# Other PSUM banks for the early softmax scores, and two softmax items a step at the end, in a fused attention, retention and feed-forward kernel

## The chip, the cores and the metric

The kernel runs on one core of a Trainium2 chip, in float32 throughout. The metric is the time on the device for one call, in microseconds (us); lower is better.

## The reference

The input is `x` with 8 sequences of 512 tokens and 256 features. Four blocks follow each other, each of them `x = x + block(layernorm(x))`: an attention with 16 heads of 16 features, a feed-forward layer (256 to 1024, relu, back to 256), a retention (scores times a decay mask, no softmax), and the same feed-forward layer again. The attention is the part that the change touches:

```python
att = jnp.einsum('bhqd,bhkd->bhqk', q, k) / jnp.sqrt(jnp.float32(HEAD_DIM))
...
att = att + (log_sparse + jnp.log(decay + 1e-09))[None, None]
att = jax.nn.softmax(att, axis=-1)
out = jnp.einsum('bhqk,bhkd->bhqd', att, v)
...
out = out + 0.2 * infini_out
```

`log_sparse` and `decay` depend on the distance of query and key alone. `q` and `k` are rotated (rope), and `k` and `v` come through a latent of 64 features.

## The kernel before, in words

The attention of one sequence is cut into four groups of four heads, so there are 32 groups. Each group is cut into 8 items: an item is 128 rows of a pair of heads against all 512 columns. That makes 256 items, and each is computed twice.

- The score item `s` has queries in rows. Two matmuls (`score_item`, L449) fill one tile of two PSUM banks, and VectorE takes the maximum of each row from it (`reduce_item`, L462, output `mr`). When a group's 8 items are through, `shift` (L470) turns the maxima with a TensorE transpose (`mx`), ScalarE negates them (`neg`), and a DMA from ScalarE's queue writes them into a spare row of `qT`.
- The softmax item `t` has keys in rows. Two matmuls (`prob_item`, L480) compute the same scores with the maximum already subtracted. ScalarE takes the exponential into a tile `p` in SBUF (`soft_item`, L493), and the tile is multiplied there with the table `dec_a` of the distance terms, half by half: on GpSimd for every third item, else on VectorE. Four such `p` tiles exist.
- `pv_item` (L504) multiplies the two items of one row block (both pairs of heads) with the values. The values carry a column of ones, so that the sum of the softmax comes out with it.

PSUM has eight banks: two score tiles `sc` of two banks each, which `s` and `t` share, one bank for `pv`, and three general banks (`misc`, L203) for everything else: layernorm transposes, latent, rope inputs, transposes of the maxima (`mx`) and of the attention's output (`num`, `aT`), output projection `wo`, feed-forward `hx` and `x`, retention `b`, `bv`, `bs`, `bo`.

One step of the main loop runs score item `t` and softmax item `t - LAG` (LAG is 10) in one burst of four matmuls, which lie on four different groups of 32 rows of TensorE. Ahead of the burst of every odd step from 13 on stands the `pv` of the two items that came last but one and last but two. The heads of an odd item are the first of that `pv`. After step 255 ten steps remain that have a softmax item alone.

All other matmul work is cut into units (class `Unit`, L280), each with a price for TensorE (`pe`) and for the engines behind it (`then`). They form chains: the front half of each sequence (layernorm, latent, k, q, rope, gates, values) and the rest of it (output projection, feed-forward, retention, feed-forward). A planner at the end of the kernel goes through the steps and decides, with clocks of its own for each engine, what stands between two steps: a unit is issued ahead of a step if it can start by the time the step can, and if a credit, which spreads the remaining work over the remaining steps, isn't used up. Its clocks only set the order. TensorE executes strictly in the order that the planner writes, as do the DMAs of the queue SP; the other engines' order within their queues is set by a scheduler from the same program. Engines wait for each other through semaphores.

The planner's own bookkeeping of the score tiles is `behind`: a step waits in the plan for the last maximum and the last exponential. The `pv` of a step is counted when the step is issued, not when it is asked when the step can start.

The early steps have little other work: the output projection of the first sequence can only start when its four groups are through, at about step 44.

## Time and profile before

| | |
|---|---|
| median of 3 runs | 1386.85 us (1384.02 to 1388.44) |
| the profiled execution | 1393.77 us |
| its span, first to last instruction | 1391.9 us |
| granted TensorE clock, mean | 0.96 |
| TensorE matmuls busy | 1286.9 us (92%) |
| VectorE busy | 805.7 us (58%) |
| ScalarE busy | 452.6 us (33%) |
| GpSimd busy | 390.5 us (28%) |

The page names instructions by what they write and read: `mr<-s` is the maximum of a score tile, `p<-t` the exponential, `p<-p,dec_a` the product with the distance table, `pv<-p,va` the product with the values. All instructions of VectorE, ScalarE and GpSimd carry line L69 and all matmuls L198 or, for transposes, L201, because small helpers issue them; so groups are told apart by tile names. `PE` is TensorE, `PEld` its weight loads, `DVE` VectorE, `ACT` ScalarE, `POOL` GpSimd, `SP` the engine that issues most DMAs. The granted clock is the share of full speed that TensorE was given.

From the page's groups of instructions, with the number of instructions, busy time and mean length of one:

| group | count | busy us | mean ns |
|---|---|---|---|
| VectorE maximum, 128x1024 | 256 | 312.7 | 1221 |
| ScalarE exponential, 128x1024 | 256 | 261.9 | 1023 |
| VectorE product with `dec_a`, 128x512 | 342 | 228.6 | 709 |
| GpSimd product with `dec_a`, 128x512 | 170 | 213.4 | 1277 |
| matmuls of `s` | 1024 | 305.6 | 680 |
| matmuls of `t` | 1024 | 301.8 | 666 |
| matmuls of `pv` | 1024 | 148.8 | 627 |

Matmul records overlap where they run on different row groups, and each float32 matmul has two records.

### The profile page before, as it was taken

To read this page: it belongs to the slowest core of one execution; us is meant where nothing else is said; L and a number is where in the kernel's file an instruction comes from. 1 tells how busy PE (TensorE), PEld (TensorE's weight loads), DVE (VectorE), ACT (ScalarE), POOL (GpSimd) and SP (SyncE) were. 2 spreads that over 40 slices of the span, in tenths; PEclk is the share of its full clock that TensorE was granted. 3 is DMA by queue.
4 is the path that set the end of the run, shared out by engine and by line. 5 is a ranking of instruction groups with operands and counts; after the bars stand their busy time and mean duration, and the time that the engine had idled before them with its cause. 6 is when DMAs were issued, how large, how long until landed. Compare 5 with 4: busy or idle time off the path is not lost.

```text
span 1391.9 us, 15456 instructions
## 1 busy us (share of the span) xinstructions
PE 1286.9 (92%) x6116; PEld 629.3 (45%) x6116; DVE 805.7 (58%) x1335; ACT 452.6 (33%) x612; POOL 390.5 (28%) x449
## 2 busy tenths in 40 slices
PE   6887799888989899898999999999999999999998
PEld 3221234343534353444535445445445454556675
DVE  4578665674584585545866667555766466524130
ACT  2133424324233324343242432433333333332211
POOL 5133341331231252213333234222432133122010
PEclk9699979998989999999999999999999999999999
DMA  5430120001200011001200030001200000000000
GB/s 130 134 62 1 27 51 1 1 1 31 47 16 1 20 36 24 16 1 31 47 1 1 5 73 16 1 0 34 44 1 1 8 8 1 1 12 4 0 16 16
DMA packets 22158, 32.08 MB, mean 23 GB/s; under 512 B 2987, under 2 KB 12652, under 8 KB 21806
## 3 DMA queue, kind: packets, MB, share of 16 engines
q1 hardware_dynamic: 21446, 30.83, 9.5%
q8 instruction: 48, 0.79, 0.2%
q10 hardware_dynamic: 640, 0.26, 0.1%
q14 instruction: 24, 0.20, 0.0%
HBM read 18.24 MB, written 12.58 MB: 22 GB/s over the span
## 4 chain that ended last, share of the span: by engine, by line
PE 66%; DVE 11%; POOL 4%; issue 3%; ACT 1%; DMA 0%; POOLq 0%; DVEq 0%; ACTq 0%
PE hx L198 15%; PE x L198 15%; PE s L198 13%; PE pv L198 6%; DVE mr L69 4%; PE wo L198 2%; PE b L198 2%; PE bs L198 2%; PE bv L198 2%; PE t L198 1%; DVE x L69 1%; PE q L198 1%; DVE p L69 1%; PE bo L198 1%; POOL p L69 1%
## 5 line engine op out<-in xcount | busy, mean ns | idle before, releaser
L69 DVE TENSOR_REDUCE mr<-s 128x2 f32<-128x1024 f32 x256 | 312.7, 1221 | 257.9 <-PE t L198 242.0
L69 ACT ACTIVATE p<-t 128x1024 f32<-128x1024 f32 x256 | 261.9, 1023 | 501.5 <-PE t L198 451.2
L69 POOL TENSOR_TENSOR p<-p,dec_a 128x512 f32<-128x512 f32 x170 | 213.4, 1277 | 545.6 <-ACT p L69 471.0
L198 PE MATMUL s<-kT,qT 32*128 32x512 f32 x1024 | 305.6, 680 | 53.2 <-DVE mr L69 48.7
L198 PE MATMUL t<-qT,kT 32*128 32x512 f32 x1024 | 301.8, 666 | 5.1 <-ACT p L69 3.8
L69 DVE TENSOR_TENSOR p<-p,dec_a 128x512 f32<-128x512 f32 x342 | 228.6, 709 | 42.6 <-ACT p L69 42.5
L198 PE MATMUL x<-w_sb,h_x 128*128 128x256 f32 x1024 | 237.2, 387 | 0.0
L198 PEld LDWEIGHTS x<-w_sb,h_x 128*128 128x128 f32 x1024 | 191.9, 191 | 61.0 <-issue 33.6
L198 PEld LDWEIGHTS s<-kT,qT 32*128 32x128 f32 x1024 | 81.7, 193 | 231.5 <-DVE mr L69 113.6
L198 PE MATMUL pv<-p,va 128*32 128x512 f32 x1024 | 148.8, 627 | 1.3 <-POOL p L69 1.1
L69 ACT ACTIVATE h_x<-hx,vec 128x512 f32<-128x512 f32 x128 | 87.8, 687 | 147.6 <-PE hx L198 146.8
L198 PE MATMUL hx<-xT_g,w_sb 128*128 128x512 f32 x256 | 122.4, 620 | 1.7 <-ACT xT_g L69 1.7
L198 PE MATMUL hx<-xT_f,w_sb 128*128 128x512 f32 x256 | 118.7, 601 | 1.2 <-ACT xT_f L69 1.1
L69 DVE TENSOR_TENSOR x<-x,x 128x256 f32<-128x256 f32 x64 | 27.1, 424 | 148.7 <-PE x L198 148.7
L198 PEld LDWEIGHTS t<-qT,kT 32*128 32x128 f32 x1024 | 79.8, 189 | 17.6 <-ACT p L69 9.2
L198 PEld LDWEIGHTS hx<-xT_g,w_sb 128*128 128x128 f32 x256 | 47.3, 195 | 68.1 <-issue 57.5
L198 PEld LDWEIGHTS hx<-xT_f,w_sb 128*128 128x128 f32 x256 | 45.5, 190 | 59.0 <-issue 52.3
L69 POOL TENSOR_TENSOR x<-x,row 128x256 f32<-128x256 f32 x64 | 54.1, 864 | 17.9 <-DVE xn_f L69 9.5
L69 POOL TENSOR_TENSOR rc<-rc,rs 128x512 f32<-128x512 f32 x32 | 39.9, 1268 | 65.0 <-DVE rc L69 48.4
L198 PEld LDWEIGHTS pv<-p,va 128*32 128x32 f32 x1024 | 22.0, 109 | 76.6 <-issue 41.8
L69 POOL TENSOR_SCALAR ve_r<-mv_r 128x2 f32<-128x2 f32 x16 | 3.6, 223 | 137.8 <-DVE mv_r L69 137.8
L198 PE MATMUL b<-xT_r,ct 128*128 128x512 f32 x64 | 32.5, 642 | 6.4 <-ACT xT_r L69 6.4
(130 smaller groups left out, 1071.6 us busy)
## 6 DMA issues: line engine op xcount, KB each, us to landing
dk<-rc SPq DMA_DIRECT2D x16, 256.0 KB
kT<-dk SPq DMA_DIRECT2D x32, 128.0 KB
dq<-rc SPq DMA_DIRECT2D x16, 256.0 KB
qT<-dq SPq DMA_DIRECT2D x32, 128.0 KB
out_dram<-x SPq DMA_DIRECT2D x32, 128.0 KB
x<-in_x_dram SPq DMA_DIRECT2D x7, 512.0 KB
w_sb<-in_w_dram SPq DMA_DIRECT2D x2, 1024.0 KB
x<-in_x_dram SPq DMA_DIRECT2D x2, 256.0 KB
```

Source lines behind the costliest of these rows:

```text
L69: ins = f(*a, **k)
L198: tc.keep_in_program_order(nc.tensor.matmul(o, lhsT=l, rhs=r, start=start, stop=stop))
```

## The change

The first 34 softmax items (`EARLY`) no longer use the score tiles. Their two matmuls write two general banks (`misc`), and ScalarE takes the exponential of each half by itself. In these steps both score tiles are free for the row maxima. Of these 34 items every even one is multiplied on GpSimd, and the odd ones on VectorE; later items are divided as before.

The ten softmax items that follow the last score item are issued two to a step, so five steps of four matmuls take the place of ten with two.

The planner's bookkeeping follows: a queue `sc` of two times stands for the two score tiles, a list `steps` gives for each step its score item, its softmax items and the item whose `pv` it carries, `step_start` now counts the wait of a `pv`, and the price of a VectorE product goes from 1680 to 1500. The order of everything that follows is planned anew with these clocks.

```diff
+    EARLY = PER + 2
...
+    def on_pool(n):
+        return n % 2 == 0 if n < EARLY else n % 3 == 2
...
-        ps = ps_sc.tile([P, 2, T], F32, tag="sc", name=f"t_{n}")
+        if n < EARLY:
+
+            ps = [misc(f"t{e}_{n}") for e in range(2)]
+        else:
+            both = ps_sc.tile([P, 2, T], F32, tag="sc", name=f"t_{n}")
+            ps = [both[:, e, :] for e in range(2)]
+            ps.append(both)
...
-        act.activation(p, ps, AF.Exp, scale=0.25)
+        if n < EARLY:
+            for e in range(2):
+                act.activation(p[:, e, :], ps[e], AF.Exp, scale=0.25)
+        else:
+            act.activation(p, ps[2], AF.Exp, scale=0.25)
...
-        eng = gps if n % 3 == 2 else dve
+        eng = gps if on_pool(n) else dve
...
+    sc = deque([0, 0])
+    steps = [(t, [t - LAG] if t >= LAG else [], t - LAG - PVLAG) for t in range(NS)]
+    steps += [(None, [n, n + 1], n - 1) for n in range(NS - LAG, NS, 2)] + [(None, [], NS - 1)]
...
     def step_start(t):
-        s = clock["PE"]
-        if t < NS:
-            s = max(s, behind["s"])
-        n = t - LAG
-        if 0 <= n < NS:
-            s = max(s, behind["t"])
-            if shifted[n // 8].done is None:
+
+        s, ts, _ = steps[t]
+        n = values_of(t)
+        at_ = clock["PE"]
+        if n is not None:
+            at_ = max(at_, prob_at[n] - 100, prob_at[n - 1] - 100)
+        own = 0
+        need = (s is not None) + sum(i >= EARLY for i in ts)
+        if need:
+            own = sc[need - 1]
+        for i in ts:
+            if i < EARLY:
+                own = max(own, banks[1])
+            if shifted[i // 8].done is None:
                 return None
-            s = max(s, shifted[n // 8].done + 2300)
-        return s
+            own = max(own, shifted[i // 8].done + 2300)
+        return max(at_, own - (1000 if n is not None else 0))
...
+            prob_at[i] = clock[e] = max(clock[e], clock["ACT"] + 60) + (2700 if on_pool(i) else 1500)
...
-    LAST = NS + LAG + PVLAG
+    LAST = len(steps)
```

More of the change, by code (lines that the diff above doesn't have):

```diff
@@ L483, in prob_item @@
         b, g = divmod(i, NG)
-        ps = ps_sc.tile([P, 2, T], F32, tag="sc", name=f"t_{n}")
+        if n < EARLY:
[4 more added lines that the diff above has]
+            ps.append(both)
         return ps, [
             (
-                ps[:, e, :], kT[b % 2][h * 32 : h * 32 + 32, g, t * P : (t + 1) * P],
+                ps[e], kT[b % 2][h * 32 : h * 32 + 32, g, t * P : (t + 1) * P],
                 qT[b % 2][h * 32 : h * 32 + 32, g, :],
@@ L724, in tile_kernel @@
     held = []
-    behind = {"s": 0, "t": 0}
-    maxed, shifted, prob_at, out_at = {}, {}, {}, {}
+    sc = deque([0, 0])
+    maxed, shifted, prob_at = {}, {}, {}
+    steps = [(t, [t - LAG] if t >= LAG else [], t - LAG - PVLAG) for t in range(NS)]
+    steps += [(None, [n, n + 1], n - 1) for n in range(NS - LAG, NS, 2)] + [(None, [], NS - 1)]
     def start_of(u):
@@ L770, in shift_unit, with values_of @@
         return u
+    def values_of(t):
+        n = steps[t][2]
+        return n if n > 0 and n % 2 == 1 else None
     def step_start(t):
-        s = clock["PE"]
-        if t < NS:
-            s = max(s, behind["s"])
-        n = t - LAG
-        if 0 <= n < NS:
-            s = max(s, behind["t"])
-            if shifted[n // 8].done is None:
-                return None
-            s = max(s, shifted[n // 8].done + 2300)
-        return s
+        s, ts, _ = steps[t]
[11 more added lines that the diff above has]
+            if shifted[i // 8].done is None:
+                return None
+            own = max(own, shifted[i // 8].done + 2300)
+        return max(at_, own - (1000 if n is not None else 0))
     def step(t):
-        n = t - LAG - PVLAG
-        if 0 <= n < NS and n % 2 == 1:
+        s, ts, _ = steps[t]
+        at_ = step_start(t)
+        n = values_of(t)
+        if n is not None:
             pv_item(n)
-            clock["PE"] = max(clock["PE"], prob_at[n], prob_at[n - 1], out_at.get(n // 8 - 1, 0)) + 1000
+            at_ += 1000
             if n % 8 == 7:
@@ L791, in step @@
                 made = Unit(None)
-                made.done = clock["PE"] + 100
+                made.done = at_ + 100
                 us[0].after.append(made)
                 posts.extend(us)
-        at_ = step_start(t)
         mms, after = [], []
-        if t < NS:
-            ps, m = score_item(t)
+        if s is not None:
+            ps, m = score_item(s)
             mms += m
-            after.append((reduce_item, t, ps))
-        n = t - LAG
-        if 0 <= n < NS:
-            ps, m = prob_item(n)
+            after.append((reduce_item, s, ps))
+        for i in ts:
+            ps, m = prob_item(i)
             mms += m
-            after.append((soft_item, n, ps))
+            after.append((soft_item, i, ps))
         for o, l, r in mms:
@@ L808, in step @@
         if mms:
-            clock["PE"] = at_ + 1080
+            at_ += 1080
+        clock["PE"] = at_
         for f, k, ps in after:
             f(k, ps)
-        if t < NS:
-            behind["s"] = maxed[t] = clock["DVE"] = max(clock["DVE"], clock["PE"] + 100) + 1280
-            if t % 8 == 7:
-                posts.append(shift_unit(t // 8))
-        if 0 <= n < NS:
-            behind["t"] = clock["ACT"] = max(clock["ACT"], clock["PE"] + 100) + 1090
-            e = "POOL" if n % 3 == 2 else "DVE"
-            prob_at[n] = clock[e] = max(clock[e], behind["t"] + 60) + (2700 if n % 3 == 2 else 1680)
+        if s is not None:
+            maxed[s] = clock["DVE"] = max(clock["DVE"], at_ + 100) + 1280
+            sc.popleft()
+            sc.append(maxed[s])
+            if s % 8 == 7:
+                posts.append(shift_unit(s // 8))
+        for i in ts:
+            if i < EARLY:
+                for e in range(2):
+                    clock["ACT"] = max(clock["ACT"], at_ + 100) + 650
+                    banks.popleft()
+                    banks.append(clock["ACT"])
+            else:
+                clock["ACT"] = max(clock["ACT"], at_ + 100) + 1090
+                sc.popleft()
+                sc.append(clock["ACT"])
+            e = "POOL" if on_pool(i) else "DVE"
+            prob_at[i] = clock[e] = max(clock[e], clock["ACT"] + 60) + (2700 if on_pool(i) else 1500)
     posts = []
```

## The prediction

> **What bounds the kernel now.** I read first the windows view, with the span cut at six points: the first score, steps 10, 44 and 50 (one maximum on VectorE is one step; I counted them along the timeline, and the cut is where the step's matmuls start), the end of the scores and the last softmax item. Columns: window, its length, busy time of PE, weight loads, VectorE, ScalarE and GpSimd, granted clock, DMA share, GB/s.

> ```profile
> 37.50:64.30 26.80, 23.65 (x60) 8.00 (x57) 16.48 (x26) 2.21 (x5) 2.42 (x5) 0.59 0.43 142
> 64.30:176.70 112.40, 85.85 (x469) 25.61 (x472) 84.82 (x115) 43.53 (x56) 38.82 (x38) 0.92 0.17 34
> 176.70:210.20 33.50, 31.85 (x141) 14.32 (x133) 21.25 (x39) 8.11 (x11) 13.98 (x16) 0.82 0.22 49
> 210.20:1203.00 992.80, 939.91 (x4654) 454.60 (x4653) 619.09 (x1012) 347.55 (x459) 290.24 (x318) 0.98 0.07 16
> 1203.00:1252.00 49.00, 47.68 (x197) 23.24 (x198) 13.22 (x25) 17.71 (x22) 10.90 (x10) 1.00 0.03 9
> 1252.00:1391.90 139.90, 132.44 (x498) 89.27 (x496) 33.69 (x89) 25.50 (x40) 16.44 (x28) 0.98 0.03 9
> ```

> From 176.7 us on TensorE is 95% busy or more. The exception is the second row, steps 10 to 43: 112.4 us for 34 steps, PE 85.9, VectorE nearly as busy. What ends PE's waits there says the waits view of that window, and how a step runs says its timeline (start, length, then the instruction, and in brackets the idle time and what ended it):

> ```profile
> PE s L198 <- DVE mr L69: 20.5, 21, 3.9
> ```

> ```profile
> 119.43 0.70 PE L198 MATMUL s<-kT,qT 32*128 32x512 f32 x2 [1.31 <-DVE mr L69]
> ...
> 120.60 1.09 PE L198 MATMUL pv<-p,va 128*32 128x512 f32 x8
> 120.61 1.23 DVE L69 TENSOR_REDUCE mr<-s 128x2 f32<-128x1024 f32 x1
> 120.71 1.02 ACT L69 ACTIVATE p<-t 128x1024 f32<-128x1024 f32 x1 [1.47 <-PE t L198]
> 121.77 1.29 DVE L69 TENSOR_TENSOR p<-p,dec_a 128x512 f32<-128x512 f32 x2
> ...
> 121.89 0.70 PE L198 MATMUL s<-kT,qT 32*128 32x512 f32 x2 [0.20 <-DVE mr L69]
> ...
> 124.34 0.70 PE L198 MATMUL s<-kT,qT 32*128 32x512 f32 x2 [0.73 <-DVE mr L69]
> ```

> Bursts of s and t start 2.46 us apart. That is 1.18 to the maximum, 1.23 for it, 0.05 back: the one score tile must be read before the next burst. The burst takes PE 1.07 (121.89 to 122.96, where the next work starts), a pv 1.0. So a step without other work leaves PE idle 1.39 when no pv lies in it (odd steps) and 0.39 when one does (even): 4.92 us a pair.

> [...] two decay products take 1.29 alone, 2.03 at 87.94 us under GpSimd's rope addition. [...]

> **The change, part by part.**

> *Scores of early softmax in other banks.* Items 0 to 33 (steps 10 to 43) take two of the three general banks, and the scores for the maxima have both score tiles. The wait of s on the last maximum goes. Next in line is pv: in the order of the built program it still stands ahead of every odd burst, and it reads the product of the odd item, which is VectorE's, made behind that step's maximum. From the rows above: burst to maximum 1.18, maximum to product 1.16 (121.77 − 120.61), product 1.29, then about 1.05 until the next burst: 4.68 a pair, against 4.92. So 17 pairs × 0.24 = 4 us. Both ends: if product and GpSimd collide (+0.74, as at 87.94) the pair is 5.4, a loss of 8 us; if ScalarE and VectorE were to flow freely, PE's 3.14 a pair plus one bank wait of 0.8 would give 3.94, a gain of 17. I take 4.68, because at that time the even item's exponential is not finished yet and GpSimd still waits for it.

> *Other PE work in these steps* (k, q, v, gates, transposes, from the built orders): 16.7 us before, 18.6 after, since k of the second batch (1.98 us) moves from step 8 to 10. The gaps of 1.39 and 0.39 hide 8.1 of it now; after the change the gap ahead of pv (4.68 − 3.14, so 1.5 a pair) hides 10.7. Left open: 8.6 and 7.9. The stage of the kernel before is then 17 × 4.92 + 8.6 = 92.2, which is 20.2 short of the 112.4 measured: the low clock, statistics and rope on VectorE ahead of a maximum (steps 20 and 21 take 5.0 each), exponentials behind the key sum. These all stay, ahead of a product instead of a maximum; but the even items no longer stand behind them. I leave 14 of the 20. After: 17 × 4.68 + 7.9 + 14 = 101.5. Gain 11, and 2 more from k leaving step 8. As a check by VectorE: six items leave it, 12 × 0.707 = 8.5, the k rope comes in, 4 × 0.74 = 3.0, so 84.8 becomes 79.3; at the same 75% busy that is 105, a gain of 7. I take **10**, ends 0 and 20.

> *Exponentials in halves.* No 128x512 exponential from PSUM is in this trace. Nearest rows: the copy of num, 0.59, relu with a bias pointer, 0.69. [...] ScalarE is busy 43.5 of 112.4, the cover: zero. Bounds: [...] 0.4 us earlier first halves on GpSimd are no gain while VectorE's product ends last. The fourth matmul of a burst waits for the exponential before it (three banks, two an item), 0.8; behind it queue pv and all PE work. It lies inside the gap of 1.5: zero; 12 us if that gap were gone.

> *Decay to GpSimd.* 17 items instead of 11: 6 × 2 × 1.27 = 15 us on an engine 38.8 busy of 112.4; behind it wait rope additions and 1/std, so k and the transposes. Zero, up to 4 lost. No DMA is added; on SP the load of batch 3 moves behind q of batch 2 and some stores behind k. DMA share 0.17 and less: zero. ScalarE's own DMA of the maxima now stands behind two halves: zero, since the planner still leaves two steps.

> *After step 44.* From here each item is again in a score tile, and 2.46 is again the floor of an empty step. But the planner has the first feed-forward at step 59 instead of 50: nine more steps lie before the large matmuls and find nothing to fill them (9.3 us of other PE work in steps 44 to 49, against 16.4). Over steps 44 to 254 I set each step's other work against its gap (1.39 odd, 0.39 even): 21.4 us uncovered before, 30.8 after, of it 0.4 and 6.3 in steps 44 to 58. In before's timeline steps without other work do show medians of 1.40 and 0.39, so the price holds. **Loss 9.4**, ends 3 and 20 (odd steps with only a maxima transpose idled 1.9).

> *Last ten items, two a burst.* Four row groups instead of two in one burst: five bursts × 1.06 = 5.3 saved, and the 1.32 ahead of the burst at 1205.38 is covered. New: pv now follows one unit after its pair. Two exponentials 2.1, then VectorE's product of the second, ready at 3.7, or GpSimd's at 4.6; the units there are 2.3 (hx and a transpose), 4.0, 3.5, 3.5, 4.0. Waits 1.4, 0, 1.1, 0.5, 0: 3.0. **Net gain 3.6**, ends 1 and 6. The 140 us behind it keep their order and their work.

> **Sum.** Against the profiled execution's span: 1391.9 − 10 − 2 + 9.4 − 3.6 = 1385.7, with the 1.9 around it 1387.6. That execution, 1393.77, is 6.9 above the median of the runs, so 1380.7: **1381**, −0.4%. About 0.3%, 4 us, is what a measurement of this kernel tells from no change.

> **Rivals.**
> - *The early gain is given back (slower).* Mechanism: after step 44 PE has no large matmuls ready for nine steps more, its clock falls there as in 168 to 206 us before, and empty steps cost up to 1.9 instead of 1.39. For it: other work thins out in the built order: 48 steps from 44 on carry less than 0.9 us of it, against 26. Against: from 410 us before idled only 33 us in 800. Price: early gain 5, loss 20, last gain 2.5 and the 2 of k: +10, so **1397**. It decides from the point where the loss exceeds 16.
> - *The wait only changes its name.* The chain through pv is 4.9 or more, because product and GpSimd collide (+0.3 suffices), and early steps give nothing but the 6 us from VectorE; loss 9.4, last 3.6: **1387**. The collision at 87.94 speaks for it, the late even exponential against.
> - *The clock stays up.* 18.5 us of steps 10 to 43 ran at half clock in the kernel before; if the denser early steps hold it and stalls fall to 6 of the 20, the gain is 18 to 20, loss 5, last 4, k 2: **1366**. Against: the statistics and rope stalls keep their place.

> **Chances.** Forecast 0.45 (own range 1375 to 1387), given back 0.27, renamed 0.13, clock 0.15. Range: 1366 to 1398; it leaves out the upper part of the second and the lower of the last. Faster: 0.36 of the forecast and nearly all of the last, 0.50; same: the renamed and 0.09 of the forecast, 0.22; slower 0.28.

> **What would show it.** In steps 10 to 43: bursts in pairs of 4.7 us, the wait of s on mr gone and one of pv on p in its place, stage near 102 us; VectorE near 79 busy. Steps 44 to 58 near 50 us with the s-on-mr wait back; from the last score (1202.93) to the end of the last pv (1256.25) it is 53.3 now; 12.6 of other work leaves this stretch for earlier steps, so about 37. I am wrong if the early stage stays above 108, if 44 to 254 lose over 15, or if that stretch idles no more than before.

## The result and the profile after

The changed kernel takes 1373.0 us (median of 4 runs, 1371.7 to 1373.4) against 1385.4 for the kernel before (4 runs, one more than shown above): ratio 0.9907, 95% interval 0.9885 to 0.993. A second set of runs of the same program, told of below, gave 1373.3 and 0.9906 [0.9888, 0.9924]. That is 12 us, 0.9%, where the prediction had 0.4%. The profiled execution took 1373.4, its span is 1371.5 and its clock 0.971. The profiled execution of the kernel before had a clock of 0.960, its other runs a median of 0.968; so 1391.9 − 1371.5 = 20.4 overstates the difference of the medians by 8.

The windows view of the kernel after, from step 10 on, with the columns of the prediction. It is cut at steps 10, 44, 59 and 76, at the last score and at the end of the last `pv`; each cut at a step lies 1.18 us ahead of that step's maximum. (TensorE itself can be up to two us ahead of such a cut.)

```profile
65.40:169.80 104.40, 94.71 (x484) 31.86 (x480) 79.51 (x103) 44.45 (x88) 55.51 (x46) 0.95 0.12 26
169.80:229.80 60.00, 48.70 (x246) 18.74 (x238) 44.87 (x77) 19.72 (x26) 26.92 (x30) 0.89 0.21 45
229.80:304.50 74.70, 70.30 (x354) 31.45 (x351) 43.88 (x65) 29.90 (x43) 17.24 (x18) 1.00 0.01 3
304.50:1197.50 893.00, 850.19 (x4219) 422.05 (x4218) 548.00 (x916) 309.95 (x410) 260.77 (x293) 0.99 0.08 18
1197.50:1235.80 38.30, 37.43 (x190) 19.02 (x186) 14.87 (x21) 14.57 (x18) 11.08 (x8) 1.00 0.03 11
```

Cut in the same places, the kernel before has:

```profile
64.60:176.90 112.30, 85.75 (x468) 25.42 (x470) 84.72 (x114) 43.53 (x56) 38.52 (x38) 0.92 0.17 34
176.90:252.40 75.50, 72.82 (x338) 33.07 (x330) 47.38 (x86) 24.11 (x31) 24.21 (x28) 0.92 0.10 22
252.40:338.10 85.70, 73.26 (x350) 31.18 (x350) 49.27 (x77) 29.58 (x42) 25.12 (x26) 0.90 0.06 13
338.10:1202.90 864.80, 825.38 (x4107) 404.60 (x4106) 543.43 (x887) 301.96 (x398) 254.89 (x280) 0.98 0.08 18
1202.90:1256.30 53.40, 52.08 (x226) 26.22 (x223) 15.01 (x29) 18.54 (x23) 10.90 (x10) 1.00 0.03 9
```

Length minus PE's busy time is idle time. The early stage (first row) falls from 112.3 to 104.4 us and its idle time from 26.6 to 9.7. (Busy includes waits inside a group of matmuls: the `pv` below is shown with 1.66 us, where one that waits for nothing takes 1.06. So not all of the idle time that went became work.) Steps 44 to 58 (second row) go from 2.7 idle to 11.3: the predicted loss. Steps 59 to 75 (third row), with nearly the same number of matmuls, go from 12.4 idle to 4.4 and from a clock of 0.90 to 1.00: this was not predicted. The last row lost 15 us, most of it because 36 matmul records of other work moved ahead of it.

The waits view of the early stage of the kernel after (engine, what it waited for: us in total, times, longest):

```profile
PE pv L198 <- DVE p L69: 8.2, 3, 6.2
PE t L198 <- DVE va L69: 1.4, 1, 1.4
```

The wait of `s` on `mr`, 20.5 us before, is gone. A `pv` that waits for VectorE's product has taken its place in the list. The timeline shows it in a step without other work:

```profile
121.32 0.70 PE L198 MATMUL s<-kT,qT 32*128 32x512 f32 x2
...
122.50 1.23 DVE L69 TENSOR_REDUCE mr<-s 128x2 f32<-128x1024 f32 x1 [1.08 <-PE t L198]
...
123.25 0.29 PEld L198 LDWEIGHTS t<-qT,kT 32*128 32x128 f32 x2 [0.60 <-ACT p L69]
123.64 1.28 DVE L69 TENSOR_TENSOR p<-p,dec_a 128x512 f32<-128x512 f32 x2
124.25 3.04 POOL L69 TENSOR_TENSOR p<-p,dec_a 128x512 f32<-128x512 f32 x2 [1.61 <-ACT p L69]
...
124.37 1.66 PE L198 MATMUL pv<-p,va 128*32 128x512 f32 x8
...
125.96 0.70 PE L198 MATMUL s<-kT,qT 32*128 32x512 f32 x2
```

Burst to maximum 1.18, maximum to product 1.14; the first heads of `pv` start at 124.37, when the first half of the product is there, and the last half carries the `pv` on to the next burst. The bursts of a pair start 2.34 and 2.30 us apart, 4.64 a pair; 4.68 was forecast. A second wait lies just under this chain: the last matmuls of the next burst, which follows at once, wait for a bank until 123.25, when ScalarE is through with the first half of a score, and end at 124.37, where `pv` starts. The product therefore carries the chain only in the last half of the `pv`, from 124.97 on. The collision of the products came as well, but it lengthened GpSimd's pair (3.04 against 2.5 alone) and left VectorE's at 1.28.

**Where the rest went: the clock.** The granted clock is either full or half in these traces: the 26 clock records of the kernel after and the 30 of the kernel before hold 1.0 and 0.5 and nothing between. Where PE has work all the time, half the clock doubles the time: in the trace of the kernel after, matmul records of `hx` follow each other every 0.853 us at half clock (median of 8) and every 0.429 at full clock (430). So time × (1 − clock) is half of the low-clock time, which is what it costs if PE has work all through it. For the medians of all runs:

| kernel | median us (runs) | ratio to before, interval | clock | time × (1 − clock) | rest |
|---|---|---|---|---|---|
| before | 1385.2 (38) | | 0.969 | 43.0 | 1341.6 |
| changed, again | 1373.3 (6) | 0.9906 [0.9888, 0.9924] | 0.973 | 37.1 | 1336.5 |
| new planner alone | 1392.5 (22) | 1.004 [1.0021, 1.0058] | 0.960 | 55.7 | 1336.5 |
| new planner and pairs | 1405.8 (6) | 1.0145 [1.0114, 1.0175] | 0.957 | 60.4 | 1346.0 |
| new planner and banks | 1371.8 (6) | 0.9886 [0.9855, 0.9917] | 0.970 | 41.2 | 1331.8 |
| old order and banks | 1382.0 (22) | 0.9979 [0.9966, 0.9993] | 0.968 | 44.2 | 1337.6 |
| changed, order as for single items | 1371.0 (6) | 0.9887 [0.9862, 0.9912] | 0.9705 | 40.4 | 1331.1 |

(Time × (1 − clock) and the rest are medians of their own, so they add up only roughly. Each ratio is to runs of the kernel before that were made beside that version; beside the three rows of the new planner these had a median of 1386.0, with 44.3 and 1341.1 in the last two columns.) Split like this the change is −5 in the rest and −6 in the clock.

The split is bookkeeping, and it overstates the clock, as PE can be waiting at half clock: of the 6.83 us of low clock from 110.5 us on in the kernel after, PE stands idle for the first 3.0. A straight line through the 38 runs of the kernel before has 0.62 us of time to 1 us of time × (1 − clock), and lines through the runs of the other versions 0.5 to 1.0. An estimate from the 0.62 is that about 4 of the 12 us are clock.

### The profile page after: what moved, and what is told of

Read it like the earlier page. It is cut to its first block, busy times and chain, and to the rows that moved or that the text cites. A ratio compares the mean times of both kernels' runs of the same rounds, so it can differ in the third digit from the quotient of the medians.

```text
span 1371.5 us, 15533 instructions
## 1 busy us (share of the span) xinstructions
PE 1279.6 (93%) x6116; PEld 632.8 (46%) x6116; DVE 795.4 (58%) x1323; ACT 453.2 (33%) x646; POOL 407.6 (30%) x461
## 5 line engine op out<-in xcount | busy, mean ns | idle before, releaser
L69 DVE TENSOR_REDUCE mr<-s 128x2 f32<-128x1024 f32 x256 | 312.7, 1222 | 269.2 <-PE t L198 255.4
L69 ACT ACTIVATE p<-t 128x1024 f32<-128x1024 f32 (+1 forms) x290 | 263.8, 923 | 496.1 <-PE t L198 447.9
L69 POOL TENSOR_TENSOR p<-p,dec_a 128x512 f32<-128x512 f32 x182 | 233.2, 1302 | 537.1 <-ACT p L69 480.9
L198 PE MATMUL s<-kT,qT 32*128 32x512 f32 x1024 | 299.2, 669 | 59.8 <-DVE mr L69 55.3
L198 PE MATMUL t<-qT,kT 32*128 32x512 f32 x1024 | 300.1, 652 | 2.7 <-DVE va L69 1.4
L69 DVE TENSOR_TENSOR p<-p,dec_a 128x512 f32<-128x512 f32 x330 | 223.9, 719 | 26.8 <-ACT p L69 26.3
L198 PE MATMUL x<-w_sb,h_x 128*128 128x256 f32 x1024 | 233.1, 383 | 0.0
L198 PEld LDWEIGHTS x<-w_sb,h_x 128*128 128x128 f32 x1024 | 190.7, 190 | 52.5 <-issue 27.6
L198 PEld LDWEIGHTS s<-kT,qT 32*128 32x128 f32 x1024 | 82.0, 191 | 228.7 <-DVE mr L69 104.5
L198 PE MATMUL pv<-p,va 128*32 128x512 f32 x1024 | 157.4, 621 | 9.5 <-DVE p L69 8.9
L69 ACT ACTIVATE h_x<-hx,vec 128x512 f32<-128x512 f32 x128 | 87.8, 688 | 152.8 <-PE hx L198 152.8
L198 PE MATMUL hx<-xT_g,w_sb 128*128 128x512 f32 x256 | 121.0, 617 | 0.7 <-ACT xT_g L69 0.7
L198 PE MATMUL hx<-xT_f,w_sb 128*128 128x512 f32 x256 | 118.9, 604 | 0.1
L69 DVE TENSOR_TENSOR x<-x,x 128x256 f32<-128x256 f32 x64 | 27.1, 423 | 154.9 <-PE x L198 154.9
L198 PEld LDWEIGHTS t<-qT,kT 32*128 32x128 f32 x1024 | 81.7, 186 | 19.9 <-ACT p L69 9.7
L198 PEld LDWEIGHTS hx<-xT_g,w_sb 128*128 128x128 f32 x256 | 47.7, 195 | 67.2 <-issue 58.1
L198 PEld LDWEIGHTS hx<-xT_f,w_sb 128*128 128x128 f32 x256 | 46.0, 191 | 58.6 <-issue 53.0
L198 PEld LDWEIGHTS pv<-p,va 128*32 128x32 f32 x1024 | 24.6, 109 | 86.7 <-issue 33.7
L69 POOL TENSOR_TENSOR rc<-rc,rs 128x512 f32<-128x512 f32 x32 | 39.9, 1268 | 69.0 <-DVE rc L69 62.1
L69 POOL TENSOR_TENSOR x<-x,row 128x256 f32<-128x256 f32 x64 | 50.3, 801 | 17.9 <-DVE xn_f L69 9.4
L69 ACT COPY num<-pv 128x512 f32<-128x512 f32 x32 | 18.7, 585 | 62.2 <-PE pv L198 62.2
L198 PE MATMUL bs<-xT_r,ret 128*128 128x512 f32 (+3 forms) x128 | 38.3, 442 | 0.0
```

What stands on the lines that cost most here:

```text
L69: ins = f(*a, **k)
L198: tc.keep_in_program_order(nc.tensor.matmul(o, lhsT=l, rhs=r, start=start, stop=stop))
```

## The experiments

**The parts alone.** First the planner without the banks, and without the pairs at the end:

```diff
-    EARLY = PER + 2
+    EARLY = 0
...
-    steps += [(None, [n, n + 1], n - 1) for n in range(NS - LAG, NS, 2)] + [(None, [], NS - 1)]
+    steps += [(None, [n], n - PVLAG) for n in range(NS - LAG, NS)]
+    steps += [(None, [], NS - 2), (None, [], NS - 1)]
```

> The new planner alone: no early banks (EARLY 0), no pairs at the end, decay products divided by thirds as before. Theory (the gain of 12 us comes from the early steps, about 8, and from the pairs at the end, about 4): no change from the kernel before, 1381 to 1389 us. Rival (the planner, which now counts the wait of a pv, orders the middle better): 1379 or less, and idle time of TensorE between steps 59 and 255 below 48 us.

Then only `EARLY = 0` (planner and pairs), and only the single items at the end (planner and banks):

> Planner and the pairs at the end, no early banks. Theory: 4 us below the planner alone (five bursts of 1.06 less, waits of pv about 1 us), so 1377 to 1385 us. Rival (the pairs only move the waits, pv behind its products): no difference from the planner alone.

> Planner and early banks, single items at the end. Theory: 8 us below the planner alone, 1373 to 1381 us, steps 23 to 42 in pairs of 4.64 us. Rival (the early gain is paid back after step 44, as fewer large matmuls stand there): within 3 us of the planner alone.

Measured: rows three to five of the table. None of the three was expected in its size. The new planner alone loses 6.5 us against the kernel before; planner and pairs lose 20; planner and banks give the whole gain of the change. In the rest column the new planner alone is 4.6 us better, so by the split its loss is clock. In its profile the loss shows in the early stage: 118.9 us, 27.9 of them at half clock. With the banks on top the rest is another 4.7 lower and the clock column 14.5. But this step is not the banks alone. The planner's clocks read `EARLY`, so it writes another order: in the traces the other matmul work differs in 191 of some 256 places between bursts, and the first feed-forward moves by six steps.

The pairs on top of the new planner alone cost 13 us. The windows view from step 208 to the last score, first with pairs, then without (two kernels, one fence each):

```profile
982.20:1227.90 245.70, 228.28 (x1134) 115.74 (x1126) 143.87 (x239) 81.80 (x105) 64.06 (x73) 0.98 0.03 7
```

```profile
978.70:1199.20 220.50, 212.32 (x1082) 105.57 (x1081) 137.93 (x225) 79.70 (x102) 61.90 (x69) 0.99 0.04 10
```

With pairs this stretch has 52 matmul records more and is idle for 17.4 us instead of 8.2. The planner spreads its credit over the steps that are left; pairs make the list shorter (262 entries instead of 268), so the credit a step rises. That this is the cause was not tested for itself; the changed kernel has the shorter list too, and its idle time from step 208 on is 8.2 us.

**Banks with the old order.** The kernel before with the early softmax in general banks and the new `on_pool`; planner and end untouched.

> The kernel before, its planner and its order of TensorE untouched, with the early banks and the alternating decay products alone. Theory (the banks and the decay on GpSimd are the gain, the new order of the work only costs): early steps 10 to 43 shorten from 112.4 to about 98 us, the rest stays: 1370 to 1376 us, as good as the whole change. Rival (the banks pay only with the order that was planned for them, since there the other work stands ahead of the waits of pv): 1379 or more.

Measured: 1382.0 us, 3 us less than before, the interval just below 1. My theory of 1370 to 1376 fell. The rival's range held (1379 or more), its reason only in part, as the banks do pay a little here. This is the one run in which banks and products change while TensorE's order stays: −4.0 in the rest, +1.2 in the clock. Pairs of steps without other work take 4.64 us here too, and the early stage of its profile is 107.9 us (98 expected), 4.5 less than before. So the banks shorten the early steps without the new order, and are worth about 3 us by themselves (1 to 5 by the interval). The rest of the 12 comes only with an order that was planned for them. How much of that is the banks, how much the order and how much the clock that falls to it, these runs don't separate: new planner with and without banks differ by 4.7 in the rest, but between planner and pairs and the changed kernel it is 9.5.

**Pairs at an equal order.** The changed kernel, with the credit spread over 268 steps, so that its order up to the last score equals that of the planner with banks and single items:

```diff
-            share = max(0, left) / max(1, LAST - t)
+            share = max(0, left) / max(1, NS + LAG + PVLAG - t)
```

> The changed kernel, its credit spread over 268 steps instead of 262, so that the order up to step 255 is that of the run with planner and early banks, and only the pairs at the end differ from that run. Theory (the pairs save 5.3 us of TensorE but pv then stands right behind its products): 0 to 4 us less than planner and early banks alone, 1368 to 1372. Rival (the pairs themselves cost, as planner and pairs without early banks was 13 us above the planner alone): 1375 or more.

Measured: 1371.0 us, 0.9 less than with single items, which the intervals don't tell from zero, and 2 less than the changed kernel. In the two profiles, the time from the last score to the end is 199.1 us with pairs and 198.4 without: the five bursts are saved, but idle time rises from 7.3 to 10.9. These two versions have the lowest medians of all.

**Who makes the product that `pv` waits for.** First, every third item on GpSimd from the beginning (`return n % 3 == 2`):

> The changed kernel with every third early decay product on GpSimd as before, instead of every second. Theory (a pair of early steps is held by maximum, VectorE's product of the odd item, pv and the burst, 4.64 us): pairs whose even item is on VectorE too get VectorE's second product into the chain, 1.3 us more in about half of the pairs, so some 6 to 10 us more than the changed kernel, 1379 to 1383. Rival (the banks are all that counts, GpSimd's share is not): 1371 to 1375.

Measured: 1379.6 us (11 runs), ratio 0.9935 [0.991, 0.996]. Pairs without other work take 4.64, 4.64 and 5.4 us in turn, the long one where the odd item is GpSimd's. An even item on VectorE didn't lengthen its pair, against what I had put down. The clock column has 46.9 and the rest 1335.2: by the split, the 6 us against the changed kernel are clock and not chain. (The planner also moved other work in three places around steps 17 to 19.)

Second, the odd items on GpSimd and the even ones on VectorE, with TensorE's order unchanged:

```diff
-        eng = gps if on_pool(n) else dve
+        eng = gps if (n % 2 == 1 if n < EARLY else n % 3 == 2) else dve
```

> The changed kernel with the same order on TensorE, and the early decay products of the odd items on GpSimd, those of the even ones on VectorE: the same load on each engine, but pv now waits for GpSimd's product of the item that came last. Theory (the early pair is a chain of burst, product of the odd item, pv): 1.3 to the exponential, 0.6 for it, 2.5 to 3.0 on GpSimd, 1.05 for pv, so pairs of 5.4 to 5.9 us instead of 4.64 and 13 to 20 us more in all. Rival (the engines' load or the three banks hold the pair at 4.64): no change, 1371 to 1375.

Measured: 1377.8 us (17 runs), ratio 0.9941 [0.9924, 0.9958]; pairs take 1.14 + 4.29 = 5.43 us. The waits view of its steps 10 to 43:

```profile
PE pv L198 <- POOL p L69: 6.5, 11, 2.7
```

The name of the engine in the wait changes with the engine of the odd item, and the pair is 0.8 longer, with the same banks and the same number of products on each engine: the product of the odd item is in the chain that sets the pace. Only steps 22 to 41 run at it: they take 54.2 us instead of 47.6. The total effect, 4.5 us, is a third of what 17 pairs would give.

**The changed kernel again**, beside these:

> The changed kernel once more, beside the others of this call: all theories 1371 to 1375 us. Its trace tells how far the low clock periods of TensorE differ from one execution to the next.

Its median is in the table. Its early stage is 107.4 us with the same 9.7 of idle time as the 104.4 above; its low-clock time there is 17.7 us instead of 11.0, and (17.7 − 11.0) / 2 is about the difference. In this stage the two executions differ by the clock alone.

**Empty steps filled.** The kernel before with ten matmuls that nothing reads, each behind the burst of one of ten odd steps between 11 and 43:

```diff
+        if t in (11, 13, 21, 25, 29, 33, 35, 37, 41, 43):
+            mm(misc(f"fill_{t}"), wq_sb[:, 0, 0, :], rope_sb[:, 0, :])
```

> The kernel before, with one extra matmul of 128x512 (about 0.9 us, its result is read by nobody) behind the burst of ten odd steps between 11 and 43 that carry no other work, where TensorE idles 1.39 us. Theory (half of the change's gain is the clock, which falls at idle gaps): the extra work costs nothing, and the clock rises above 0.969 on average, so 1380 to 1385 us. Rival (the clock does not react to gaps as short as these): clock 0.968 to 0.969 as before, time the same or up to 5 us more, 1385 to 1390.

Measured: 1387.1 us (22 runs), ratio 0.9995 [0.9978, 1.0012], clock 0.9695 against 0.968 for before in the same comparison. The early stage was 112.0 us long and its wait of `s` on `mr` fell from 20.5 to 9.8 us: the gaps of 1.39 hide such matmuls almost entirely. My theory fell: the time did not change, and the clock column is only 2 us lower (42.3 against 44.3).

**More early items.** `EARLY` of 50 and of 66 instead of 34, in the version with the credit over 268 steps:

> The run with pairs and early banks in the same order as planner and early banks, but the banks and the alternating decay for 50 items instead of 34, so that the steps up to 59 run without the wait for the one score tile; the planner then has the first feed-forward at step 52. Theory (the idle 11 us in steps 44 to 58 is the return of that wait): it falls to about 4, 1362 to 1368 us. Rival (the three banks are needed there for the output projection and rope, and the plan as a whole decides): 1369 or more.

> The same with 66 items, up to step 75. There nearly every step carries large matmuls, which need the general banks too. Theory: no more gain than with 50 items, as the gaps there are filled anyway and the softmax halves take two of three banks from the feed-forward: 0 to 8 us more than with 50. Rival (the double score tile helps everywhere): 3 us less or better.

Measured: 1386.9 us (14 runs; 0.9989 [0.9968, 1.0009]) and 1379.3 (22 runs; 0.994 [0.9923, 0.9957]), against 1371.0 at 34. Both theories fell (the ranges of the rivals held). Idle time did become less, in steps 44 to 58 to 4.4 us as expected at 50, in all 85.1 us against 90.4 at 34, and the rest is 1332.5 against 1331.1; but the clock column has 53.4 instead of 40.4. By the split the clock takes 13 of the 16 us at 50, and 3 of the 8 at 66, where 4 more are in the rest. The planner reads `EARLY` here too: from step 44 on the other work lies elsewhere in 179 places, so these runs don't tell the number of items from the order.

**What a low clock follows.** So less idle time need not mean less time. The windows view, cut every 3.41 us, shows what stands ahead of a low clock. Kernel after:

```profile
342.63:346.04 3.41, 3.41 (x22) 1.15 (x20) 2.30 (x7) 1.43 (x2) 2.36 (x5) 1.00 0.00 0
346.04:349.46 3.42, 0.99 (x9) 0.31 (x8) 2.85 (x6) 0.18 (x1) 2.04 (x3) 1.00 0.00 0
349.46:352.87 3.41, 3.41 (x20) 1.77 (x16) 2.26 (x4) 1.61 (x2) 1.85 (x2) 0.50 0.02 5
352.87:356.28 3.41, 2.68 (x24) 1.04 (x20) 1.91 (x3) 1.50 (x2) 0.64 (x1) 1.00 0.00 0
```

Kernel before:

```profile
308.40:311.81 3.41, 0.84 (x8) 0.42 (x4) 3.16 (x6) 0.00 (x0) 2.88 (x4) 1.00 0.00 0
311.81:315.22 3.41, 2.12 (x5) 0.59 (x5) 1.23 (x2) 0.88 (x3) 2.55 (x4) 0.50 0.00 0
315.22:318.64 3.42, 2.16 (x6) 0.50 (x4) 1.92 (x3) 2.10 (x5) 0.59 (x2) 0.50 0.52 155
318.64:322.05 3.41, 3.41 (x18) 0.72 (x16) 0.51 (x1) 1.02 (x1) 2.08 (x2) 0.50 0.00 0
322.05:325.46 3.41, 2.08 (x16) 0.83 (x12) 2.96 (x4) 1.44 (x2) 0.41 (x1) 1.00 0.61 104
```

A window in which PE was busy 0.99 of 3.41 us is followed by one at half clock; the next, at 2.68 (78%), by none. In the kernel before the windows behind those of 2.12 and 2.16 at half clock are low too, and the one behind a full one is not. The places to cut come from the clock records of the traces: in the kernel after and in the kernel before, all changes of the clock inside the span lie within 0.03 us of one grid of 3.413 us, and the low stretches are 3.41, 6.83, 10.24, 13.65, 23.89 and 30.72 us long (1, 2, 3, 4, 7 and 9 steps of it). The offset of the grid differs from execution to execution: from the first instruction to its first line it is 1.2 us in the kernel before, 1.3 in the kernel after and 1.8 in its second execution. Counted over all 14 traces of this study: of the windows that are recorded at full clock, 121 of 134 that were busy less than half were followed by a low one, 56 of 477 that were busy 50 to 80%, and 2 of 4594 above that. Of the low windows after the first 62 us, 53 of 53 that were busy less than 80% were followed by another low one, 16 of 23 between 80 and 90%, and 30 of 178 above. (Some matmul records can be missing, so single windows may be misjudged.)

The second execution of the changed kernel ("again" in the table) tests this without any edit. The window with 0.99 us above holds a stall of 2.43 us ahead of step 84. In the second execution the same stall lies across two windows:

```profile
346.56:349.97 3.41, 1.83 (x12) 0.68 (x4) 2.22 (x8) 1.38 (x2) 2.37 (x5) 1.00 0.00 0
349.97:353.39 3.42, 2.57 (x24) 1.33 (x24) 3.42 (x6) 1.26 (x2) 1.07 (x3) 1.00 0.00 0
```

No low window follows, and from burst 83 to burst 86 it takes 10.17 us instead of 11.75. The program and the stall are the same, the place of the grid is not, and the execution with the low window takes 1.6 us more here.

This reads the runs above. Gaps of 1.39 and 0.39 in 4.92 us leave PE 64% busy on average, and of the windows that were busy 50 to 80% only 56 of 477 were followed by a low one; filling the gaps changed little. For one stall of 2 to 2.4 us, whole in one window, my estimate is up to half of the 3.41 us of the window behind it on top of itself; at step 84 it was the 1.6. A test by intervention, the changed kernel with matmuls that nothing reads, meant for its longest stalls:

```diff
+    FILL = {23: 6, 44: 1, 51: 2, 53: 1, 82: 1, 83: 2, 98: 2, 104: 2, 119: 2, 150: 1, 158: 2, 168: 2, 200: 2, 240: 3}
...
+            mm(o, wq_sb[:, 0, 0, :], rope_sb[:, 0, :])
```

> The changed kernel with 28 matmuls of 128x512 that nothing reads, put where TensorE stands idle longest in its trace: six ahead of the pv of step 23 (idle 6.2 us), three ahead of the burst of step 240 (3.0 to 4.0), one or two ahead of the bursts of steps 44, 51, 53, 82, 83, 98, 104, 119, 150, 158, 168 and 200 (1.7 to 2.4). The computation and the order of all else stay. Theory: the low clock is granted by windows of 3.41 us on a fixed grid: in the traces so far 90 of about 110 such windows in which TensorE was busy less than half were followed by a low one, and of those busy over 80% hardly any. The stalls named stand ahead of about 34 of the 79 us of low clock in the changed kernel; filled, they take away 20 to 34 us of it, so 8 to 15 us of time: 1358 to 1366 us, clock of the runs 0.98 or more instead of 0.972. Rival one: the clock follows the mean load, to which 24 us more of matmul in 1371 add little: 1371 to 1376, clock 0.970 to 0.975. Rival two: the extra matmuls come late, because they wait for a general bank, and push the bursts back: 1376 to 1385.

Measured: 1389.1 us (14 runs), ratio 1.0003 [0.9986, 1.0019], 16 us more than the changed kernel; clock 0.977 instead of 0.973. Low-clock time in the trace is 59.8 us instead of 78.7 and 78.1. But 7 to 10 us of this difference lie before step 22, ahead of the first of these matmuls; behind it there are 29.0 us instead of 41.2 and 37.1, so 8 to 12 went, not the 20 to 34 expected.

The trace shows that nine of the fourteen places are one burst too early: the stalls stand ahead of steps 45, 52, 54, 84, 105, 120, 159, 169 and 201, the matmuls ahead of the bursts before these. (The others are where they were meant to be: ahead of the `pv` of step 23, and of steps 82, 98, 150 and 240. `FILL` sums to 29 matmuls, not 28.) At step 159 even the misplaced ones pushed the burst back far enough to break up the stall. First the kernel after, then this one:

```profile
701.04:704.45 3.41, 1.00 (x12) 0.26 (x8) 2.18 (x4) 0.48 (x1) 1.11 (x3) 1.00 0.00 0
704.45:707.86 3.41, 3.41 (x10) 0.91 (x7) 2.12 (x3) 1.02 (x1) 0.59 (x1) 0.50 0.00 0
```

```profile
707.95:711.36 3.41, 3.14 (x16) 0.99 (x14) 2.01 (x6) 2.17 (x3) 1.77 (x4) 1.00 0.00 0
711.36:714.78 3.42, 3.01 (x14) 1.19 (x15) 2.78 (x4) 1.02 (x1) 0.68 (x1) 1.00 0.00 0
```

In both executions of the changed kernel a low window follows this stall of 2.4 us. Here the stall is 0.68 us and none follows, and bursts 157 to 162 take 30.2 us instead of 31.8. So here, as in the counts above, the low clock goes with the load of the window ahead of it (1.00 us busy of 3.41, against 3.14); the mean load, 93% in the kernel after and 94% here, hardly differs.

The time went up for two reasons. The second rival holds at step 23. Its waits view and timeline:

```profile
PE fill L198 <- DVE atok L69: 7.3, 1, 7.3
```

```profile
111.11 6.83 PE L198 MATMUL fill<-rope_sb,wq_sb 128*128 128x512 f32 x12 [7.34 <-DVE atok L69]
117.87 1.06 PE L198 MATMUL pv<-p,va 128*32 128x512 f32 x8
```

The six ahead of step 23 wait for a general bank until the stall is over, then run, the first four of twelve records at half clock (0.50 from 107.23 to 114.05), and push `pv` back: steps 22 and 23 take 5.5 us more. The larger part is the misplacing: around steps 51, 104, 168 and 200 the bursts that were pushed back led to new waits for an exponential or a product, and cost 2.6 to 4.9 us each, 15.5 together; around 104 and 200 a low window came that was not there before. At the four places ahead of steps 82, 98, 150 and 240, where the matmuls stand in the stall itself, nothing became slower. Of 29.6 us of added matmuls only 10 lie in what was idle time (91.9 in the kernel after, 82.0 now). The rest column rises from 1336.5 to 1356.2, the clock column falls from 37.1 to 31.9. The run missed its forecast of 1358 to 1366; whether matmuls right in the stalls would reach it stays open.

## Why the prediction was right, and where it was off

- **Direction, mechanism of the early steps and range held**: faster, 12 us instead of 6, and 1373 lies between 1366 and 1398. Without the clock the sum was −10 − 2 + 9.4 − 3.6 = −6.2; the rest column has −5.1. That they are so near is luck, and hangs on how the clock is split off: the sum had more gain in the early steps than was measured (10 for 5 to 8), more loss after step 44 (9.4 for 4.0 of idle time) and more from the pairs (3.6 for 0.9), and these errors cancel. The range was 32 us wide, too, for a change of 12.
- **The early pair** was right: 4.64 us for 4.68, `pv` on VectorE's product in the place of `s` on `mr`. That the product is in the chain is shown by the kernel with odd items on GpSimd (5.43), that the banks bring the pair without the new order by the kernel with old order and banks (4.64).
- **The early stage, "I leave 14 of the 20"**: too little. 104.4 − 17 × 4.64 − 7.9 = 17.6, and 20.6 in the second execution. Only steps 22 to 41, counted by their maxima, run at the pace of the pair, 47.6 us instead of 59.4; steps 10 to 21 take 47.8 instead of 44.9. The largest stall is now the 6.21 us ahead of the `pv` at 113.47. There VectorE normalizes the next sequence, and that waits 1.16 us for GpSimd's 1/std and then runs beside GpSimd's product (2.61 us from 109.08 on; the pair ahead of it, at 106.10, took 1.67). The stage gained 8 us (5 in the second execution, 4.5 with the old order) instead of 10.
- **"−2 from k leaving step 8"**: hardly seen in the time. From the first score to step 10 it is 26.1 us instead of 26.9; this stretch runs at half clock for all of its length in the kernel after, for 21.5 us in the kernel before, which by an estimate (half of the 4.6 us more) can have hidden about 2.
- **"Loss 9.4" after step 44**: idle time in steps 44 to 254 rose from 54.5 to 58.5, 4.0 in all. Steps 44 to 58 lost 8.6, more than the 5.9 for them in the sum, and took 60 us instead of "near 50". But steps 59 to 75 gave back 8.0. The method had set other work against its gap step by step; it didn't count waits that a new order removes, such as those of `s` and `mx` on `mr` in steps 59 to 75.
- **"Net gain 3.6" for the pairs**: 38.3 us from the last score to the last `pv` for "about 37". But at an equal order they are worth 0.9 and perhaps nothing: the waits behind them take what the bursts save. In the changed kernel the shorter list of steps moves the other work; it is 2 us slower than that version (within the intervals).
- **The clock**, which the forecast took as unchanged: this is the term that was missing, −6 of the 12 by the split, about −4 by the estimate above. The rival "The clock stays up" named it but put it in the wrong place. Low-clock time in steps 10 to 43 is 11.0 and 17.7 us in two executions against 18.7; in steps 59 to 75 it goes from 17.1 to 0, in steps 76 to 107 from 17.1 to 3.4 and to 0.

The prediction's rivals tied the clock to thin and dense stages as a whole. The traces show it by single windows: one stall of 2.43 us inside one window of 3.42 us (346.04 to 349.46) was followed by a low one.

Left open: a version that fills each stall at its own place, without taking a general bank, was not tried, nor a `pv` two steps later, which would need more `p` tiles. The order of the changed kernel without the banks was not run either, so its own share of the 12 us isn't known. How much of the 56 in 477 is due to missing records is not known.

## What to carry to other kernels

Look at the clock before reading a measured time as the effect of an edit: time × (1 − clock) beside the rest, as a bound and not as a price. And where a planner decides, compare the orders in the traces: turning off one part here also changed the order of everything else, so the versions "without banks" were no test of the banks alone. When PE must idle, many short gaps (1.39 and 0.39 us) cost little more than their own length here: ten of them filled took 2 us off the clock column (42.3 for 44.3) and nothing off the time. One stall of 2.43 us came with 1.6 us more in one of two executions, so breaking up the long stalls comes first. (No run here gained time by it yet.) A matmul that is to fill a stall must stand right at it: one burst earlier it pushed the real work back here, by 2.6 to 4.9 us at four places. Where a bank or tile wait is removed, look for the next instruction in the engine's written order and work out the chain behind it: here that gave the new pace of the early steps to 1% (4.68 us a pair forecast, 4.64 measured).

## What the runs showed of the hardware

```profile
136.61 2.49 POOL L69 TENSOR_TENSOR p<-p,dec_a 128x512 f32<-128x512 f32 x2 [3.00 <-ACT p L69]
...
138.11 2.15 DVE L69 TENSOR_TENSOR p<-p,dec_a 128x512 f32<-128x512 f32 x2
```

- Two half exponentials of 128x512 from PSUM took 1.09 us together, one of 128x1024 1.02.
